# 3x3 convolution of two bottleneck layers: last row tile by F(2,3), three of six row combinations with four products per two columns, differences on GpSimd, statistics on ScalarE

## The chip, the cores and the metric

The kernel runs on one core of a Trainium2 chip. The metric is the time of one execution on the device in microseconds, the median of several runs; lower is better. Everything is float32. TensorE (PE) does the matrix products, VectorE (DVE) element work between tiles, ScalarE (ACT) function evaluations and copies, GpSimd (POOL) slow element work, and SyncE (SP) issues transfers.

## The reference

Two residual bottleneck layers in a row, on an input of 64 images, 1024 channels, 14 x 14 pixels:

```
for layer in range(2):
    h = relu(bn(conv1x1(x, w1) + b1))        # 1024 -> 256 channels
    h = relu(bn(conv3x3(h, w2, pad=1) + b2)) # 256 -> 256
    h = bn(conv1x1(h, w3) + b3)              # 256 -> 1024
    x = relu(x + softplus(residual_scale) * h)
```

`bn` takes mean and variance of each channel over all 64 x 14 x 14 pixels of the batch. So no value of a layer's next step can be made before all images of the step ahead are done and their statistics are known.

## The kernel before

The stages follow each other: conv1 of layer 0 (to about 310 us), the 3x3 convolution of layer 0 (to 655), a Gram stage that derives the statistics of conv3 from a matrix of inner products (to 773), conv3 of layer 0 fused with conv1 of layer 1 (to about 1380), the 3x3 convolution of layer 1 (to about 1730), its Gram stage, and conv3 with the residual to the end. Within a stage each engine works through its own list in a fixed order that a scheduler sets when the program is built; engines wait for each other by semaphores. The results of conv1 and conv2 stay in SBUF as one tensor `y`, 128 partitions x 2 halves of the channels.

The change lies in the 3x3 convolution, `conv2`, and in `filters`, which prepares its weights. `conv2` computes in place over `y`, in NG = 8 groups of GI = 8 images. It is a Winograd scheme in both directions:

- Rows: the 14 output rows are cut into RT = 4 tiles of four rows, the last with two that count. F(4,3) makes four output rows from NF = 6 *combinations* i of input rows. `combine` builds them on VectorE (tiles `r`), the fourth tile's row with help from ScalarE (`last`, L420). They are handled in pairs: (1,2), then (3,4), then (0,5). A combination has 4 x 8 = 32 lines of 14 columns, combination 5 only 24.
- Columns: F(2,3) with five products per two output columns. Even and odd columns are kept as two halves of a line. `sums` (L437) holds the two halves added. In `products`, L494 multiplies `sums` with the shared weight D1D2 into one PSUM bank, and L513 multiplies the halves with D1, D3, D2 and D0 into two more. Each of these exists for two halves of the input channels and two of the output channels: 20 products to a combination. One float32 product is two rows in the trace.
- `finish`: ScalarE copies the shared bank to `ms` (L535, or L531 with the bias for combination 1). VectorE adds it to the two other banks (`column`, L541), giving `f`, then builds output rows from the six `f` by the inverse row transform (L563 to L583), writes them over `y`, and takes batch statistics of each row tile (`bn_stats`, L555). `summarize` and `aggregate` join the statistics of all groups.

The loop over pairs issues the row combinations of the next pair ahead of the products of this one:

```
now, ahead = ahead, combine(*pairs[k + 1]) if k + 1 < len(pairs) else None
acc = finish(g, pair, products(now, k == 0), acc)
```

PSUM has eight banks and all serve this stage in turn, three to a combination, so a bank is taken again after eight takings, when its last reader is done. The transformed weights `u` of a combination come from DRAM for every group by SyncE's queue, three buffers deep. `norm` (L401) applies conv1's normalization and relu to the next group on ScalarE.

`filters(b, s, o, spare)` transforms one quarter of the 3x3 weights of layer b and writes the six sets to DRAM by GpSimd's queue. Layer 0's four quarters are done beside conv1 of layer 0, layer 1's beside the Gram stage of layer 0.

Of the kernel before, what the change touches and what calls it, by code (L numbers as in the profile page):

```python
# [34 lines left out]
P = 128  # L36
# [21 lines left out]
RT, NF, NK = 4, 6, 5  # L58
LINE = GI * W
BUFS = dict(u=3, t=3, r=4, sums=4, ms=3, f=2)  # L60
D0, D1D2, D3, D1, D2 = range(NK)
# [11 lines left out]
def bottlenecks(ctx: ExitStack, tc: tile.TileContext, x, w1s, w2s, w3s, pars, out):  # L73
# [10 lines left out]
        [dram.tile([P, MS, MS, NK, P], FP, tag=f"u{b}_{i}", name=f"u{b}_{i}") for i in range(NF)] for b in range(2)  # L84
# [61 lines left out]
    def filters(b, s, o, spare):  # L146
# [13 lines left out]
        n = NK * P  # L160
        for i in range(NF):

            u = second[:, (i - 1) * n : i * n] if 0 < i < NF - 1 else first[:, 3 * w :][:, (2 * w if i == 0 else 0) :]
            u = u[:, :n].rearrange("p (k m) -> p k m", k=NK)
            r = u[:, 0:3, :].rearrange("p k m -> p (k m)")
            if i in (0, NF - 1):
                nc.scalar.activation(r, g[:, 0 if i == 0 else 2], AF.Copy, scale=0.25 if i == 0 else 1.0)
            else:
                base, by = ((even, -1.0 / 6), (even, 1.0 / 6), (quad, 1.0 / 12), (quad, -1.0 / 12))[i - 1]
                nc.vector.scalar_tensor_tensor(r, g[:, 1], by, base, ALU.mult, ALU.add)  # L170
            nc.vector.tensor_sub(
                u[:, D1 : D2 + 1], u[:, D0 : D3 + 1 : D3 - D0], u[:, D1D2 : D1D2 + 1].to_broadcast([P, 2, P])
            )
            nc.gpsimd.dma_start(out=us[b][i][:, s, o], in_=u)
# [233 lines left out]
    def conv2(psum, pool, b, par, aff, stats):  # L408
        pairs = [(g, p) for g in range(NG) for p in ((1, 2), (3, 4), (0, NF - 1))]
# [15 lines left out]
        def combine(g, pair, between=None):  # L425


            full = RT - 1
# [3 lines left out]
            def ready(r):  # L432
                i = pair[len(made)]
                lines = (full if i == NF - 1 else RT) * GI
                r = r.rearrange("p s r (i w) -> p s (r i) w", i=GI)[:, :, :lines]
                sums = pool.tile([P, MS, RT * GI, WH], FP, tag="sums", name="sums", bufs=BUFS["sums"])[:, :, :lines]
                nc.vector.tensor_add(sums, r[:, :, :, WH:], r[:, :, :, :WH])  # L437
                u = pool.tile([P, MS, MS, NK, P], FP, tag="u", name="u", bufs=BUFS["u"])
                nc.sync.dma_start(out=u, in_=us[b][i])
                made.append((i, lines, r, sums, u))  # L440

            both = slice(0, MS)
            if pair[0] == 1:
                t1, t2 = new("t"), new("t")
                slots = [both] if between is None else [slice(s, s + 1) for s in range(MS)]
                for part in slots:
                    if part.start:
                        between()
                    last(t1, g, 2, -4.0, part)
                    last(t2, g, 1, -4.0, part)  # L450
# [4 lines left out]
                ready(ra)  # L455
                nc.vector.tensor_sub(rb, t1, t2)
                ready(rb)
            elif pair[0] == 3:
                t3, t4 = new("t"), new("t")
                last(t3, g, 2, -1.0)  # L460
                last(t4, g, 1, -1.0)
                for t, k in ((t3, 4), (t4, 3)):
                    ins = nc.vector.tensor_sub(
                        t[:, :, :full], rows(g, both, k, 0, full), rows(g, both, k - 2, 0, full)
                    )
                    if g == 0:
                        tc.keep_in_program_order(ins)
                stt(ra, t4, 2.0, t3)
                ready(ra)
                stt(rb, t4, -2.0, t3)  # L470
                ready(rb)
            else:
                last(ra, g, 2, -5.0)
                for s in range(MS):
                    stt(ra[:, s, :full], rows(g, s, 2, 0, full), -5.0, rows(g, s, 4, 0, full))
                    stt(rb[:, s, :full], rows(g, s, 3, 0, full), -5.0, rows(g, s, 5, 0, full))
                for s in range(MS):
                    stt(ra[:, s, 1:], rows(g, s, 0, 1, RT), 4.0, ra[:, s, 1:])
                    stt(rb[:, s, :full], rows(g, s, 1, 0, full), 4.0, rb[:, s, :full])
                ready(ra)  # L480
                ready(rb)
            return made

        def products(made, first):
# [3 lines left out]
            for i, lines, r, sums, u in made:  # L488
                n = lines * WH
                m = psum.tile(2 * RT * GI * WH).rearrange("p (o n) -> p o n", o=MS)  # L490
                eos = [psum.tile(2 * RT * GI * WH).rearrange("p (q n) -> p q n", q=2) for o in range(MS)]

                def shared(o, s):
                    nc.tensor.matmul(  # L494
                        m[:, o, :n], u[:, s, o, D1D2], sums[:, s].rearrange("p l c -> p (l c)"),
# [3 lines left out]
                def columns(o, s, part):  # L499

                    odd, even = (eos[o][:, q, :n].rearrange("p (l c) -> p l c", c=WH) for q in range(2))
                    to, k, v = (
# [13 lines left out]
                if by_slot:  # L516
                    order = [(s, o, part) for s in range(MS) for o in range(MS) for part in range(4)]
                    order += [(s, o, None) for o in range(MS) for s in range(MS)]
                else:
                    order = [  # L520
                        (s, o, part) for o in range(MS) for part in (None, 0, 1, 2, 3) for s in range(MS)
                    ]
                for s, o, part in order:
                    if part is None:
                        shared(o, s)
                    else:
                        columns(o, s, part)
# [6 lines left out]
                else:  # L534
                    nc.scalar.activation(ms[:, :, :n], m[:, :, :n], AF.Copy)  # L535
# [421 lines left out]
```

## Time and profile before

| | |
|---|---|
| median of 3 runs | 2176.95 us (2176.35 to 2179.06) |
| profiled execution, its own time | 2176.9 us |
| its span | 2175.1 us |
| 3x3 convolution of layer 0, about | 310 to 655 us |
| Gram stage of layer 0, about | 655 to 773 us |
| 3x3 convolution of layer 1, about | 1380 to 1730 us |

A profile row names the source line, the engine, the operation, the written and read tiles, and the shapes. Busy times of engines overlap, so they don't add up to the span. What a change in a stage is worth is read from which engine has no gaps there.

### The profile page before, as it was taken

Reading aid. Unit: us, or ns where it says so; the run is one execution under the profiler, and the core shown is the slowest. Engines: PE = TensorE matmul, PEld = TensorE weight load, DVE = VectorE, ACT = ScalarE, POOL = GpSimd, SP = SyncE. Lnnn points to the kernel's source line nnn. Section 1 sums busy time; section 2 is a strip of 40 time slices with the busy share of each in tenths; the row PEclk is TensorE's granted clock in tenths of the full one; section 3 lists DMA queues with packets and bytes.
Section 4 is the critical chain, followed back from the end, with each engine's and each line's share of the span. In section 5 each row is a group of like instructions: output and inputs, shape, how many; then the busy total and the mean of one; then the engine's idle time right before and its main releaser. Section 6 shows DMA issues by size and latency. Waiting matters only on the chain.

```text
span 2175.1 us, 27250 instructions
## 1 busy us (share of the span) xinstructions
PE 2123.2 (98%) x10624; PEld 1802.2 (83%) x10624; DVE 1432.1 (66%) x2648; ACT 720.8 (33%) x1387; POOL 243.6 (11%) x342
## 2 busy tenths in 40 slices
PE   8999989999998999999999999899999899999999
PEld 4555559999997879999999999899999897555555
DVE  5666567788775667667667666778878634444444
ACT  1111124111105045555555555611111221444444
POOL 0000000000001123333333333000000000000000
PEclk9999999999999999999999999999999999999999
DMA  7655524555544434444444443355555411777885
GB/s 285 252 203 208 177 102 173 190 194 194 192 147 164 156 119 167 164 174 171 160 174 178 178 171 126 151 194 194 188 181 194 185 47 53 303 296 292 299 300 233
DMA packets 45010, 409.45 MB, mean 188 GB/s; under 512 B 5584, under 2 KB 5840, under 8 KB 12240
## 3 DMA queue, kind: packets, MB, share of 16 engines
q1 hardware_dynamic: 30528, 288.67, 36.8%
q0 software_dynamic: 8448, 67.11, 7.5%
q10 hardware_dynamic: 5904, 51.91, 5.8%
q8 instruction: 84, 1.38, 0.3%
q14 instruction: 46, 0.38, 0.1%
HBM read 289.18 MB, written 118.49 MB: 187 GB/s over the span
## 4 chain that ended last, share of the span: by engine, by line
PE 93%; DVE 3%; DMA 1%; ACT 1%; issue 0%; POOL 0%; SPq 0%; DVEq 0%; ACTq 0%
PE ps L513 23%; PE ps L144 17%; PE ay L144 15%; PE cy L144 8%; PE ap L144 8%; PE ps L494 6%; PE ax L144 4%; PE cp L144 4%; PE cp L622 4%; PE cx L144 2%; PE ap L623 2%; PE ps L640 1%; DMA y<-in_w 1%; DVE spare L170 0%; ACT y L401 0%
## 5 line engine op out<-in xcount | busy, mean ns | idle before, releaser
L513 PE MATMUL ps<-r,u 128*128 128x224 f32 (+3 forms) x3072 | 561.3, 334 | 14.1 <-DVE r L454 14.1
L513 PEld LDWEIGHTS ps<-r,u 128*128 128x128 f32 x3072 | 535.1, 189 | 19.8 <-DVE r L454 7.9
L144 PE MATMUL ps<-y,w 128*128 128x392 f32 x1024 | 339.5, 494 | 0.0
L144 PEld LDWEIGHTS ps<-y,w 128*128 128x128 f32 x1024 | 195.4, 191 | 143.0 <-issue 1.9
L704 DVE SCALAR_TENSOR_TENSOR x<-ps,scale,x 128x392 f32<-128x392 f32 x256 | 160.1, 626 | 174.4 <-PE ps L144 174.4
L239 ACT ACTIVATE cu<-cy,scale 128x196 f32<-128x196 f32 x372 | 154.0, 423 | 221.2 <-PE cy L144 221.2
L705 ACT ACTIVATE x<-x,shift 128x392 f32<-128x392 f32 x264 | 163.7, 622 | 182.8 <-DVE x L704 182.8
L144 PE MATMUL ay<-at,w1s 128*128 128x196 f32 (+1 forms) x752 | 209.7, 382 | 1.2 <-ACT au L239 1.0
L541 DVE TENSOR_TENSOR f<-ps,ms 128x448 f32<-128x448 f32 x192 | 111.2, 598 | 128.4 <-PE ps L513 73.7
L494 PE MATMUL ps<-sums,u 128*128 128x224 f32 (+1 forms) x768 | 169.7, 344 | 0.0
L535 ACT ACTIVATE ms<-ps 128x448 f32<-128x448 f32 (+1 forms) x80 | 42.0, 525 | 382.6 <-PE ps L494 382.6
L144 PEld LDWEIGHTS ay<-at,w1s 128*128 128x128 f32 x752 | 136.0, 190 | 36.6 <-ACT au L239 4.6
L239 ACT ACTIVATE x<-x,shift 128x392 f32<-128x392 f32 x248 | 140.9, 614 | 27.9 <-POOL x L373 27.9
L373 POOL TENSOR_TENSOR x<-x,cu 128x392 f32<-128x392 f32 x124 | 125.9, 1015 | 187.6 <-DVE x L347 187.6
L347 DVE SCALAR_TENSOR_TENSOR x<-cp,scale,x 128x196 f32<-128x196 f32 x248 | 103.5, 417 | 63.7 <-PE cp L144 63.7
L494 PEld LDWEIGHTS ps<-sums,u 128*128 128x128 f32 x768 | 136.5, 189 | 0.1
L622 PE MATMUL cp<-zt 128*128 128x257 f32 x392 | 119.9, 387 | 6.5 <-DVE zt L642 6.2
L144 PE MATMUL cy<-ct,w3s 128*128 128x196 f32 x496 | 123.0, 330 | 1.4 <-ACT cu L239 1.4
L239 ACT ACTIVATE au<-ay 128x196 f32<-128x196 f32 (+1 forms) x141 | 53.8, 381 | 178.4 <-PE ay L144 175.8
L144 PE MATMUL ap<-x,w1s 128*128 128x196 f32 (+1 forms) x376 | 107.7, 390 | 4.9 <-DVE y L285 4.9
L401 ACT ACTIVATE y<-y,shift,scale 128x1568 f32<-128x1568 f32 (+2 forms) x68 | 103.1, 1585 | 5.6 <-DVE shift L801 5.6
L144 PE MATMUL ay<-x,w 128*128 128x196 f32 (+1 forms) x376 | 104.8, 381 | 0.0
(188 smaller groups left out, 3056.5 us busy)
## 6 DMA issues: line engine op xcount, KB each, us to landing
u<-u SPq DMA_DIRECT2D x96, 1280.0 KB, 5.5
x<-in_x SPq DMA_DIRECT2D x62, 1568.0 KB, 6.7
x<-mid SPq DMA_DIRECT2D x32, 1568.0 KB, 8.6
mid<-x ACTq DMA_DIRECT2D x31, 1568.0 KB, 5.1
out<-x POOLq DMA_DIRECT2D x31, 1568.0 KB, 7.7
u<-y POOLq DMA_DIRECT2D x24, 320.0 KB, 6.6
u<-spare POOLq DMA_DIRECT2D x24, 320.0 KB, 3.1
y<-in_w SPq DMA_DIRECT2D x4, 576.0 KB, 8.7
```

Of the source, the lines that this page charges most:

```text
L144: tc.keep_in_program_order(nc.tensor.matmul(*args, **kw))
L239: tc.keep_in_program_order(nc.scalar.activation(*args, **kw))
L347: nc.vector.scalar_tensor_tensor(v, bank, self.scale[:, o : o + 1], v, ALU.mult, ALU.add)
L373: nc.gpsimd.tensor_add(v, v, self.u12)
L401: nc.scalar.activation(y, y, AF.Relu, bias=shift[:, s : s + 1], scale=scale[:, s : s + 1])
L494: nc.tensor.matmul(m[:, o, :n], u[:, s, o, D1D2], sums[:, s].rearrange("p l c -> p (l c)"), start=(s == 0), stop=(s == MS - 1),)
L513: nc.tensor.matmul(to, u[:, s, o, k], v, start=start, stop=stop, skip_group_check=by_slot)
L541: nc.vector.tensor_tensor(f[:, o].rearrange("p r (i q c) -> p q (r i) c", i=GI, q=2)[:, :, :lines], eos[o][:, :, :n].rearrange("p q (l c) ...
L622: nc.tensor.matmul(g0, zt[:, c, 0:P], zt[:, c, :], start=first, stop=last)
L623: nc.tensor.matmul(g1, zt[:, c, P:M], zt[:, c, P:], start=first, stop=last)
L704: nc.vector.scalar_tensor_tensor(v, ps, scale[:, o : o + 1], v, ALU.mult, ALU.add)
L705: nc.scalar.activation(v, v, AF.Relu, bias=shift[:, o : o + 1])
```

## The change

1. The last row tile, of which two rows count, is made by F(2,3) instead of F(4,3). It needs combinations 0, 1, 2 and 5 only, so combinations 3 and 4 have 24 lines now, and combination 5 has 32. The factors of `last` change, and the fourteenth output row is written apart (L671).
2. Combinations 3, 4 and 5 (`FOUR`) use a column scheme with four products per two columns: weights D0M2, SUM, DIFF and D3M1. `sums` goes with SUM, a new operand `diffs` with DIFF, and a new operand `v` with the other two, always over all seven columns of a half. That is 16 products (32 rows) instead of 20 (40 rows), and four PSUM banks instead of three (`less` beside `m` and the two of `eos`). `diffs` is made by GpSimd (L478); `v` by two operations of VectorE (L482) and two of ScalarE for the end columns (L486, L487). In `finish`, `shared_part` (L619) writes `m - ms` and `m + ms` to `f` by two operations of VectorE before the columns (L627) are added.
3. Statistics: groups 0 and 7 keep `bn_stats`. For groups 1 to 6, ScalarE reads the finished group twice per channel half with an accumulated output (`moment`, L700: Identity and Square around a center that group 0 gives), after the pairs (1,2) and (3,4) of the next group. `merge` and `begin` bring the three parts into six entries.
4. The last pair is handled as (5, 0).
5. `filters` makes the four weights of `FOUR` combinations by more and smaller operations, and these sets have 1024 KB instead of 1280.

```
-        pairs = [(g, p) for g in range(NG) for p in ((1, 2), (3, 4), (0, NF - 1))]
+        pairs = [(g, p) for g in range(NG) for p in ((1, 2), (3, 4), (NF - 1, 0))]
...
-                lines = (full if i == NF - 1 else RT) * GI
+                lines = (full if i in (3, 4) else RT) * GI
...
                 nc.vector.tensor_add(sums, r[:, :, :, WH:], r[:, :, :, :WH])
+                if i in FOUR:
+                    diffs = half("diffs")
+                    nc.gpsimd.tensor_sub(diffs, r[:, :, :, :WH], r[:, :, :, WH:])
+                    v = pool.tile([P, MS, RT * GI, W], FP, tag="v", name="v", bufs=BUFS["v"])[:, :, :lines]
+                    for s in range(MS):
+                        q = r[:, s].rearrange("p l (q c) -> p l q c", q=2)
+                        nc.vector.tensor_sub(
+                            v[:, s, :, 1 : W - 1].rearrange("p l (q c) -> p l q c", q=2),
+                            q[:, :, :, 1:], q[:, :, :, : WH - 1],
+                        )
+                    nc.scalar.activation(v[:, :, :, 0], r[:, :, :, 0], AF.Copy)
+                    nc.scalar.activation(v[:, :, :, W - 1], r[:, :, :, W - 1], AF.Copy, scale=-1.0)
+                    r = v
...
+                if four:
+                    for to, k, v in ((less, DIFF, diffs), (m, SUM, sums)):
+                        for o, s in each:
+                            shared(to, k, v, o, s)
+                    for o in range(MS):
+                        for part in range(2):
+                            for s in range(MS):
+                                columns(o, s, part)
...
+        def shared_part(item, f):
+            four, lines, m, ms, eos = item
+            if four:
+                a, l = (v[:, :, : lines * WH].rearrange("p o (l c) -> p o l c", c=WH) for v in (m, ms))
+                for q, op in enumerate((ALU.subtract, ALU.add)):
+                    nc.vector.tensor_tensor(halves(f, lines)[:, :, q], a, l, op)
...
+        def moment(g, o, k):
+            nc.scalar.activation(
+                idle, y_all[:, o, g * GPX : (g + 1) * GPX], (AF.Identity, AF.Square)[k], bias=center[:, o : o + 1],
+                accum_out=moments[:, o, k, g - 1 : g],
+            )
...
+            if g > 1 and pair[0] in (1, 3):
+                for i in range(2):
+                    moment(g - 1, (1, 3).index(pair[0]), i)
...
+            if i in FOUR:
+                r0, r1, r2 = (row[:, k * P : (k + 1) * P] for k in range(3))
+                ends = rest[:, w : w + P]
+                nc.vector.tensor_add(ends, r0, r2)
+                nc.vector.tensor_add(u[:, SUM], ends, r1)
+                nc.vector.tensor_sub(u[:, DIFF], ends, r1)
+                nc.scalar.activation(u[:, SUM : DIFF + 1], u[:, SUM : DIFF + 1], AF.Copy, scale=0.5 * by)
+                nc.scalar.activation(u[:, D0M2], r0, AF.Copy, scale=-by)
+                nc.scalar.activation(u[:, D3M1], r2, AF.Copy, scale=by)
```

What follows is the order of instructions on an engine at three places, without times. First TensorE: one output half of combination 3 or 4 before.

```order
L494 MATMUL ps<-sums,u 128x224 x2
L513 MATMUL ps<-r,u 128x224 x2
L513 MATMUL ps<-r,u 128x32x6 x2
L513 MATMUL ps<-r,u 128x224 x2
L513 MATMUL ps<-r,u 128x32x6 x2
```

And after, for the whole combinations 3, 4 and 5 in turn:

```order
L550 MATMUL ps<-diffs,u 128x168 x4
L550 MATMUL ps<-sums,u 128x168 x4
L560 MATMUL ps<-v,u 128x168 x8
L550 MATMUL ps<-diffs,u 128x168 x4
L550 MATMUL ps<-sums,u 128x168 x4
L560 MATMUL ps<-v,u 128x168 x8
L550 MATMUL ps<-diffs,u 128x224 x4
L550 MATMUL ps<-sums,u 128x224 x4
L560 MATMUL ps<-v,u 128x224 x8
```

The shared products, of `diffs` and of `sums`, now stand ahead of all column products of a combination instead of ahead of each output half's.

Second VectorE, in the finish of the pair (3, 4) of an early group. Before (L541 is `column`, L456 the combination 4 of the next group, L423 the two-operand form `stt`):

```order
L541 TENSOR_TENSOR f<-ps,ms 128x2x32x7 x2
L456 TENSOR_TENSOR r<-t 128x896
L568 TENSOR_TENSOR fc<-f 128x896
L569 TENSOR_TENSOR fd<-f 128x896
L423 SCALAR_TENSOR_TENSOR y<-fc,fa 128x3x112
L423 SCALAR_TENSOR_TENSOR y<-fd,fb 128x4x112 x2
L423 SCALAR_TENSOR_TENSOR y<-fc,fa 128x3x112
L423 SCALAR_TENSOR_TENSOR fb<-fd,fb 128x2x336
L573 TENSOR_TENSOR fa<-fa,fc 128x896
L555 BN_STATS stats_0_1195<-y 128x6 x4
```

After (L619 is the shared part, L482 `v` of combination 5, L627 `column`):

```order
L475 TENSOR_TENSOR sums<-r 128x448
L619 TENSOR_TENSOR f<-ps,ms 128x2x24x7 x2
L482 TENSOR_TENSOR v<-r 128x32x12 x2
L627 TENSOR_TENSOR f<-ps,f 128x2x24x7 x2
L513 TENSOR_TENSOR t<-y 128x2x336
L619 TENSOR_TENSOR f<-ps,ms 128x2x24x7 x2
L475 TENSOR_TENSOR sums<-r 128x448
L627 TENSOR_TENSOR f<-ps,f 128x2x24x7 x2
L457 SCALAR_TENSOR_TENSOR r<-t 128x2x336
L652 TENSOR_TENSOR fc<-f 128x2x336
L653 TENSOR_TENSOR fd<-f 128x2x336
```

The statistics are gone from this place, and shared parts and `v` stand ahead of the columns.

Third ScalarE, between two groups. Before (L420 are last rows of `t` and `r`, L535 and L531 the copies to `ms`):

```order
L420 ACTIVATE t<-y 128x2x112 x2
L535 ACTIVATE ms<-ps 128x448
L535 ACTIVATE ms<-ps 128x2x168
L531 ACTIVATE ms<-ps,par_134 128x224 x2
L420 ACTIVATE t<-y 128x2x112 x2
L420 ACTIVATE r<-y 128x2x112
```

After (L454 are the last rows, L486 and L487 end columns of `v`, L700 the moments, L605 and L601 the copies):

```order
L605 ACTIVATE ms<-ps 128x448
L486 ACTIVATE v<-r 128x2x24
L487 ACTIVATE v<-r 128x2x24
L454 ACTIVATE t<-y 128x2x112
L700 ACTIVATE idle,moments<-y,center 128x1568
L454 ACTIVATE r<-y 128x2x112
L700 ACTIVATE idle,moments<-y,center 128x1568
L454 ACTIVATE r<-y 128x2x112
L700 ACTIVATE idle,moments<-y,center 128x1568
L601 ACTIVATE ms<-ps,par_134 128x224 x2
L700 ACTIVATE idle,moments<-y,center 128x1568
L605 ACTIVATE ms<-ps 128x448
```

Three moments now stand ahead of the copy of combination 1's shared product, with last rows between them.

More of the change, by code (lines that the diff above doesn't have):

```diff
@@ L83, in bottlenecks @@
     us = [
[L84 removed]
+        [dram.tile([P, MS, MS, NKS[i], P], FP, tag=f"u{b}_{i}", name=f"u{b}_{i}") for i in range(NF)]
+        for b in range(2)
     ]
@@ L160, in filters @@
         n = NK * P
+        rest = first[:, 5 * w + n :]
+        bases = {1: (even, -1.0 / 6), 2: (even, 1.0 / 6), 3: (quad, 1.0 / 12), 4: (quad, -1.0 / 12)}
         for i in range(NF):
[L163 to L167, printed above, removed]
-            else:
-                base, by = ((even, -1.0 / 6), (even, 1.0 / 6), (quad, 1.0 / 12), (quad, -1.0 / 12))[i - 1]
-                nc.vector.scalar_tensor_tensor(r, g[:, 1], by, base, ALU.mult, ALU.add)
```

218 lines of the change are left out of this document (142 added, 76 removed).

## The prediction

> **What bounds the kernel now.** I read the page's totals and its chain first, then one steady group of eight images by stretches of time, then that group's products and vector work one by one, last the waits.
>
> ```profile
> PE 2123.2 (98%) x10624; PEld 1802.2 (83%) x10624; DVE 1432.1 (66%) x2648; ACT 720.8 (33%) x1387; POOL 243.6 (11%) x342
> ...
> PE 93%; DVE 3%; DMA 1%; ACT 1%; issue 0%; POOL 0%; SPq 0%; DVEq 0%; ACTq 0%
> PE ps L513 23%; PE ps L144 17%; PE ay L144 15%; PE cy L144 8%; PE ap L144 8%; PE ps L494 6%; PE ax L144 4%; PE cp L144 4%; PE cp L622 4%; PE cx L144 2%; PE ap L623 2%; PE ps L640 1%; DMA y<-in_w 1%; DVE spare L170 0%; ACT y L401 0%
> ```
>
> TensorE holds 93% of the chain, and the products that the change cuts (L494, L513) hold 29% of it.
>
> ```profile
> core 0: us, PE busy (x) PEld busy (x) DVE busy (x) ACT busy (x) POOL busy (x), PEclk, DMA share, GB/s
> 406.56:448.14 41.58, 41.58 (x242) 41.30 (x241) 33.83 (x59) 5.14 (x12) 0.00 (x0) 1.00 0.53 190
> 310.00:655.00 345.00, 337.70 (x1927) 333.87 (x1926) 276.08 (x486) 67.63 (x117) 0.00 (x0) 0.99 0.50 183
> 655.30:773.00 117.70, 104.73 (x657) 92.63 (x658) 65.45 (x137) 34.45 (x36) 13.10 (x28) 0.95 0.41 148
> ```
>
> The first row is one steady group of the 3x3 convolution. It takes 41.58 us and TensorE has no gap in it; VectorE works 33.83 us, ScalarE 5.14, GpSimd not at all. So each microsecond of products saved is a microsecond of the group, until VectorE stands in the way. Its room is 41.58 - 33.83 = 7.75 us now, and the change shrinks that from above.
>
> ```profile
> DVE f L541 <- PE ps L513: 37.6, 24, 1.7
> DVE f L541 <- ACT ms L535: 26.9, 17, 4.3
> PE ps L513 <- DVE r L454: 7.3, 1, 7.3
> ```
>
> In the whole first 3x3 stage the only large wait of TensorE is the one at its start (7.3 us, once); VectorE is the one that waits, for products and for ScalarE's copy of them.
>
> **TensorE: narrower and fewer products.**
>
> ```profile
> 434.55 0.92 PE L494 MATMUL ps<-sums,u 128*128 128x224 f32 x4
> ...
> 438.16 0.92 PE L494 MATMUL ps<-sums,u 128*128 128x224 f32 x4
> ...
> 441.77 0.73 PE L494 MATMUL ps<-sums,u 128*128 128x168 f32 x4
> 442.34 2.32 PE L513 MATMUL ps<-r,u 128*128 128x168 f32 x16
> 444.50 0.73 PE L494 MATMUL ps<-sums,u 128*128 128x168 f32 x4
> ...
> 447.22 0.92 PE L494 MATMUL ps<-sums,u 128*128 128x224 f32 x4
> ```
>
> From one L494 to the next is one output half of a combination: 20 rows in the trace, 4 of L494 and 16 of L513, half of the latter without the last column. With 32 lines that is 12 x 224 + 8 x 192 = 4224 columns in 3.61 us, 0.855 ns a column; with 24 lines 12 x 168 + 8 x 144 = 3168 columns in 2.73 us, 0.862. A group is now 5 x 7.22 + 5.45 = 41.6 us, as the window says.
>
> After, combinations 0, 1 and 2 keep 7.22 us each. Combinations 3 and 4 have 24 lines and 32 full rows: 32 x 168 x 0.862 = 4.63 us each. Combination 5 has 32 lines and 32 rows: 32 x 224 x 0.855 = 6.13. Sum 21.7 + 9.26 + 6.13 = 37.08, so 4.51 us less a group and **72.2 us** less over 16 groups (eight in each layer).
>
> **VectorE: what is swapped.** Time from start to start in the same group:
>
> ```profile
> 412.73 1.14 DVE L541 TENSOR_TENSOR f<-ps,ms 128x448 f32<-128x448 f32 x2
> 413.80 0.91 DVE L423 SCALAR_TENSOR_TENSOR r<-y 128x336 f32<-128x336 f32 x2
> 414.63 0.92 DVE L423 SCALAR_TENSOR_TENSOR r<-y,r 128x336 f32<-128x336 f32 x2
> ...
> 422.25 1.08 DVE L564 TENSOR_TENSOR fb<-f 128x896 f32<-128x896 f32 x1
> 423.26 0.50 DVE L423 SCALAR_TENSOR_TENSOR r<-y 128x336 f32<-128x336 f32 x1
> ...
> 440.20 0.85 DVE L423 SCALAR_TENSOR_TENSOR fb<-fd,fb 128x672 f32<-128x672 f32 x1
> 440.97 1.08 DVE L573 TENSOR_TENSOR fa<-fa,fc 128x896 f32<-128x896 f32 x1
> ```
>
> 448 elements take 1.07 / 2 = 0.535 us, 336 take 0.415, 896 take 1.01, 672 take 0.77. That is 1.04 ns an element and 0.07 us, so 288 would be 0.37, 384 0.47, 224 0.30. Per steady group the change removes eight statistics (4 x 0.535 + 4 x 0.415 = 3.80). It adds the differences `v` (4 x 0.37 + 2 x 0.47 = 2.42), the shared parts of L619 (4 x 0.415 + 2 x 0.535 = 2.73), the fourteenth row apart (0.30), and a wider sum and columns of combination 5 (0.36). Three rows instead of four in combinations 3 and 4 and in what is built from them take off some 2.16. Net -0.15: about 33.7 us of work in a group of 37.08. Nine tenths busy, still not the bound.
>
> Does its order hold up TensorE? In the order of after, VectorE's tightest stretch begins with the second column of combination 2, which can't run before TensorE has ended that combination, 14.46 us into the group. Behind it stand r, fa, fb, sums, combination 3's shared part and combination 5's `v`; by the pitches above these are done at about 19.4 and 20.3. TensorE, with four banks for a combination of four products instead of three, asks for the bank that this shared part frees at 25.25, and for `v` at 26.8. Slack 5.9 us. In group 0 of each layer the statistics stay on VectorE and L619 and `v` come on top, so it needs 39 us and hands group 1 a lateness of 2 to 5 us, less than that slack. I take 1 us for both layers (0 to 6).
>
> **GpSimd: the differences.** Two operands of 336 elements twice and of 448 once per group. The fused stage has the nearest rows:
>
> ```profile
> L373 POOL TENSOR_TENSOR x<-x,cu 128x392 f32<-128x392 f32 x124 | 125.9, 1015 | 187.6 <-DVE x L347 187.6
> L368 POOL TENSOR_TENSOR x<-x,cu x124: 596/600/1117, 786.5 to 1366.2; 128x196 f32<-128x196 f32 x124
> ...
> 786.18 0.96 DVE L312 TENSOR_TENSOR at<-x,at 128x784 f32<-128x784 f32 x1
> ...
> 786.49 1.12 POOL L368 TENSOR_TENSOR x<-x,cu 128x196 f32<-128x196 f32 x1 [2.07 <-ACT cu L239]
> ```
>
> 196 elements take 0.600 us and 392 take 1.015: 2.1 ns an element and 0.19 us, so 2 x 0.90 + 1.13 = 2.93 us a group. The result is wanted a pair of combinations later, so GpSimd's own time is hidden by products. But the last two rows show one add starting inside a VectorE operation with two inputs in SBUF, and taking 1.12 instead of 0.60. The two engines can hold each other up, so VectorE may lose anything from 0 to those 2.93 us; at the worst 33.7 + 2.9 = 36.6, still under 37.08. Nothing in the sum, but no room left: this is the first rival.
> [...]
>
> **ScalarE: the statistics.**
>
> ```profile
> L401 ACT ACTIVATE y<-y,shift,scale 128x1568 f32<-128x1568 f32 x58 | 93.9, 1684 | 2.8 <-DVE shift L801 2.8
> L420 ACT ACTIVATE t<-y 128x224 f32<-128x224 f32 x60 | 20.0, 381 | 64.2 <-DVE r L456 55.6 <-DVE r L423 8.6
> ```
>
> The four moments of a group have the size of L401's row, 93.9 / 58 = 1.62 us each, and the end columns of `v` are small, like L420 (six a group, 0.3 to 0.4). 5.14 + 6.5 + 2 is some 13 to 14 us of 37. What matters is the queue: three moments stand between the last-row copies that VectorE needs and combination 1's `ms`. From the moment U that allows the first, the copy for combination 5 ends at about U + 4.7 and VectorE reaches it at U + 5.7; `ms` comes at U + 6.7, VectorE's column at U + 6.5. Cost 0.2 us of VectorE, none of TensorE.
>
> **Weights and the stages beside.**
>
> ```profile
> u<-u SPq DMA_DIRECT2D x45, 1280.0 KB, 5.5
> ...
> PE cp L622 <- DVE zt L642: 6.2, 5, 1.6
> L171 DVE TENSOR_TENSOR spare<-spare 128x256 f32<-128x256 f32 x24 | 9.0, 417 | 1.4 <-ACT spare L167 1.4
> ...
> 652.97 2.32 PE L513 MATMUL ps<-r,u 128*128 128x168 f32 x16
> 661.33 1.30 PE L640 MATMUL cy<-ident,y 128*128 128x128 f32 x4 [6.05 <-ACT y L401]
> ```
>
> A load of weights lands in 5.5 us, three buffers give it more than 9 us, and those of four products have a fifth less to bring: nothing. The filters are transformed beside other stages, layer 0's four pieces in the first, layer 1's in the Gram stage (655 to 773 us). Each piece gets six more operations of VectorE (three of 128 elements for one of 256, +0.8 us) and eight small copies of ScalarE more (+2.2 us). In the Gram stage TensorE already waits for VectorE five times, 6.2 us in all: +2 us there (0 to 4 x 3.0 = 12, if all were exposed), +0.5 in the first. After the last product TensorE has 6.05 us of nothing while statistics end; the last item is now 448 wide instead of 336, three operations longer by 0.12 each: +0.4 a layer, +0.8.
>
> **Sum.** The profiled execution took 2176.9 us (span 2175.1), the same as the median. 2176.9 - 72.2 + 1 + 2.5 + 0.8 = **2109 us**. By ends: without the added terms 2105, with them all at their upper ends 2124.
>
> **Rivals.**
> 1. *VectorE becomes the bound.* The differences read at a stride, the adds of the fused stage don't. If they take 1.12 / 0.60 = 1.87 times as long and block VectorE throughout, it needs 33.7 + 5.5 = 39.2, which is 2.1 over TensorE. Seven boundaries give 14.8 less 5.9 slack, so about 9 a layer: 2127; with half of the blocking it stays at 2109. For it speaks the 1.12 row; against it that blocking in full needs every difference to lie beside VectorE work of two SBUF inputs.
> 2. *The change loses (the other side).* The same lock, but each difference holds VectorE over 2.6 us: (41.6 - 33.7) / 3 is the point from which a group is longer than now. At 3.0 us a group is 42.7: 2176.9 + 1.1 x 16 + 4 = 2199. Against it: 2.6 us is more than twice the slowest add, 1.12.
> 3. *The narrow products gain less.* If rows of 168 were paced by their weight loads, 32 x 0.188 = 6.02 us instead of 4.63, the saving falls to 1.73 a group, 27.7 in all: 2153. Against it:
>
> ```profile
> L513 PEld LDWEIGHTS ps<-r,u x3072: 187/188/338, 319.6 to 1724.7; 128*128 128x128 f32 x192
> 442.20 2.24 PEld L513 LDWEIGHTS ps<-r,u 128*128 128x128 f32 x16
> ```
>
> One load lasts 188 ns, but sixteen beside rows of 168 and 144 take 2.24 us, 140 ns each: they overlap.
> 4. *The filters are exposed.* Each piece holds up its stage for its whole 3.0 us, in both stages: +24 less the 2.5 taken: up to 2130.
>
> **Chances.** The forecast 0.70, with a range of its own of 2104 to 2116; the first rival 0.18; the filters 0.06; weight loads 0.03; the loss 0.03. All but the last are faster by more than 0.2% (4.4 us, about what a measurement of this kernel can tell from no change); a partial loss that ends within it gets 0.01. 2102 to 2130 holds all but the third and the second rival; its low end lets the narrow rows run at 0.855 ns a column (1.2 us less) and leaves room for the spread of the runs (2176.35 to 2179.06).
>
> **What would show it.** Right: a group period near 37.1 us with TensorE at 97% or more; the L550 and L560 rows of 168 columns at 0.145 us each; differences of 0.9 to 1.15 us; moments at 1.6; the Gram stage within 2 us of 117.7. Wrong: in the 3x3 stages TensorE waits for shared parts or `v`, VectorE busy above 95%, L619 or `v` much over 0.42 us beside GpSimd's work (first rival); narrow rows at 0.188 (third); more than 10 us of waits for `zt` in the Gram stage (fourth).

## The result, and the profile after

The changed kernel takes 2128.55 us (median of four runs, 2126.36 to 2129.66) against 2176.65 before; the ratio is 0.9775 with a 95% interval of 0.9758 to 0.9792. That is 48.1 us less where 68 were forecast. The profiled execution took 2126.36 us, its span 2124.6, which is 50.5 less than the span before.

First the page of after, the lines that answer to those of before, and the new GpSimd group (count, then busy time and mean ns of one, then idle time before it):

```profile
PE 2058.2 (97%) x10240; PEld 1733.5 (82%) x10240; DVE 1466.6 (69%) x2826; ACT 823.3 (39%) x1627; POOL 355.5 (17%) x390
...
PE 92%; DVE 5%; ACT 2%; issue 1%; DMA 1%; POOL 0%; DVEq 0%; POOLq 0%; ACTq 0%; SPq 0%
...
L478 POOL TENSOR_TENSOR diffs<-r 128x336 f32<-128x336 f32 (+1 forms) x48 | 112.1, 2337 | 622.4 <-DVE r L457 394.0
```

TensorE is busy 65.0 us less (2123.2 to 2058.2), and VectorE and ScalarE together have gained three points of the chain. The differences take 2.34 us each on the average, more than twice the 0.98 that was forecast.

Next, where the time went. These are the starts of the stages in the timeline of after, then of before; L863 and L730 are the same line, the first VectorE work for conv3:

```profile
344.78 8.44 PE L573 MATMUL ps<-r,u 128*128 128x224 f32 x32 [7.30 <-DVE r L506]
649.25 1.40 PE L773 MATMUL cy<-ident,y 128*128 128x128 f32 x4 [6.12 <-ACT y L427]
L863 DVE TENSOR_TENSOR ct<-ct,y x31: 356/410/412, 758.2 to 1330.8; 128x196 f32<-128x196 f32 x31
1376.86 7.82 PE L573 MATMUL ps<-r,u 128*128 128x224 f32 x32 [6.80 <-DVE r L506]
1679.36 1.39 PE L773 MATMUL ps<-ident,y 128*128 128x128 f32 x4 [4.77 <-ACT y L427]
```

```profile
319.62 8.74 PE L513 MATMUL ps<-r,u 128*128 128x224 f32 x32 [7.30 <-DVE r L454]
L730 DVE TENSOR_TENSOR ct<-ct,y x31: 354/410/413, 773.1 to 1344.8; 128x196 f32<-128x196 f32 x31
1390.81 7.36 PE L513 MATMUL ps<-r,u 128*128 128x224 f32 x32 [6.81 <-DVE r L454]
1729.89 1.39 PE L640 MATMUL ps<-ident,y 128*128 128x128 f32 x4 [4.79 <-ACT y L401]
```

Subtracting neighbours (the Gram stage of layer 0 began at 661.33 before) gives this table, in us:

| stage | before | after | difference |
|---|---|---|---|
| conv1 of layer 0, to the first product of the 3x3 | 319.6 | 344.8 | +25.2 |
| 3x3 of layer 0, with its tail | 341.7 | 304.5 | -37.2 |
| Gram stage of layer 0 | 111.8 | 109.0 | -2.8 |
| fused conv3 and conv1 | 617.7 | 618.7 | +1.0 |
| 3x3 of layer 1, with its tail | 339.1 | 302.5 | -36.6 |
| the rest | 445.2 | 445.2 | 0.0 |

So the 3x3 stages gave 73.8 us, and conv1 of layer 0, which the change touches only through the filter pieces beside it, took 25 of them back.

One steady group of after, on TensorE (start, duration, then the instruction and how many in a row):

```profile
435.70 1.30 PE L550 MATMUL ps<-diffs,u 128*128 128x168 f32 x8
436.84 1.30 PE L550 MATMUL ps<-sums,u 128*128 128x168 f32 x8
437.98 2.48 PE L560 MATMUL ps<-v,u 128*128 128x168 f32 x16
440.30 1.30 PE L550 MATMUL ps<-diffs,u 128*128 128x168 f32 x8
...
444.89 1.67 PE L550 MATMUL ps<-diffs,u 128*128 128x224 f32 x8
...
450.98 0.92 PE L550 MATMUL ps<-sums,u 128*128 128x224 f32 x4
```

A combination of 24 lines takes 440.30 - 435.70 = 4.60 us (forecast 4.63) and combination 5 takes 450.98 - 444.89 = 6.09 (6.13). The windows over four groups of after and five of before, in the columns of the prediction's window, say how full the engines are:

```profile
444.89:592.70 147.81, 147.81 (x866) 146.91 (x865) 138.76 (x255) 48.14 (x99) 33.63 (x12) 1.00 0.54 193
```

```profile
406.56:614.46 207.90, 207.90 (x1202) 206.51 (x1201) 170.12 (x293) 25.44 (x59) 0.00 (x0) 1.00 0.52 190
```

147.81 / 4 = 36.95 us a group against 41.58, with TensorE still without a gap. VectorE works 34.7 us of that (34.0 of 41.58 before), ScalarE 12.0.

Now the stage that became longer. TensorE, with what it waited for, then its waits in the first 330 us:

```profile
47.60 2.80 PE L155 MATMUL ay<-at,w 128*128 128x392 f32 x8
55.13 5.17 PE L155 MATMUL ay<-at,w1s 128*128 128x392 f32 x8 [4.74 <-ACT au L265]
60.14 2.80 PE L155 MATMUL ax<-x,w 128*128 128x392 f32 x8
```

```profile
PE ay L155 <- ACT au L265: 19.5, 5, 4.7
```

`au` (L265) is ScalarE's copy of a bank that TensorE is to go on using. It comes 4.74 us late once for each of the four filter pieces. ScalarE's own list at that place shows why, and then VectorE's:

```profile
50.77 0.29 ACT L193 ACTIVATE y<-y 128x128 f32<-128x128 f32 x1
53.33 0.42 ACT L191 ACTIVATE y<-y 128x256 f32<-128x256 f32 x1 [2.27 <-DVE y L190]
53.99 0.31 ACT L192 ACTIVATE y<-y 128x128 f32<-128x128 f32 x1 [0.25 <-DVE y L183]
54.21 0.49 ACT L193 ACTIVATE y<-y 128x128 f32<-128x128 f32 x2
54.61 0.47 ACT L265 ACTIVATE au<-ay 128x392 f32<-128x392 f32 x1
```

```profile
51.11 1.78 DVE L338 TENSOR_TENSOR at<-x,at 128x1568 f32<-128x1568 f32 x1
52.81 0.28 DVE L189 TENSOR_TENSOR y<-y 128x128 f32<-128x128 f32 x1
53.01 0.28 DVE L190 TENSOR_TENSOR y<-y 128x128 f32<-128x128 f32 x1
53.40 0.56 DVE L183 SCALAR_TENSOR_TENSOR y<-y 128x384 f32<-128x384 f32 x1
```

TensorE had filled the bank at about 50.4. But ahead of `au` in ScalarE's list stood L191, a small copy of a filter, which waited 2.27 us for VectorE's L190, and that stood behind a sum `at` of 1.78 us. Then came L192 and two L193, of which the first two needed L183. L183 writes the scratch that both combinations use, so it stands behind L190, the last of VectorE's sums that read it for the combination ahead. `au` itself waited for nothing by 54.61; it was only behind.

The stall cost more than its length: the eight products after it took 5.17 us instead of the 2.80 of the next eight. The windows over the stall and over these products have the reason, in the third number from the end, the granted clock:

```profile
50.30:55.10 4.80, 0.10 (x1) 0.00 (x0) 4.59 (x11) 2.03 (x8) 1.32 (x3) 0.77 0.95 345
55.10:60.50 5.40, 5.37 (x10) 2.90 (x11) 1.10 (x4) 1.07 (x3) 1.08 (x2) 0.57 0.77 242
```

Over the stretch behind the stall the granted clock was 0.57, and 0.50 in its first 2.9 us. So a piece cost about 4.7 us of waiting and 2.4 us of slow products.

### The profile page after: what moved, and what is told of

It is laid out like the page before. It is cut to its first block, busy times and chain, and to the rows that moved or that the text cites. A ratio compares the mean times of both kernels' runs of the same rounds, so it can differ in the third digit from the quotient of the medians.

```text
span 2124.6 us, 27204 instructions
## 1 busy us (share of the span) xinstructions
PE 2058.2 (97%) x10240; PEld 1733.5 (82%) x10240; DVE 1466.6 (69%) x2826; ACT 823.3 (39%) x1627; POOL 355.5 (17%) x390
## 4 chain that ended last, share of the span: by engine, by line
PE 92%; DVE 5%; ACT 2%; issue 1%; DMA 1%; POOL 0%; DVEq 0%; POOLq 0%; ACTq 0%; SPq 0%
PE ps L155 17%; PE ay L155 15%; PE ps L573 13%; PE ps L550 9%; PE cy L155 8%; PE ap L155 7%; PE ps L560 6%; PE ax L155 4%; PE cp L155 4%; PE cp L755 3%; PE cx L155 2%; PE ap L756 2%; ACT y L427 1%; PE ps L773 1%; DVE at L319 0%
## 5 line engine op out<-in xcount | busy, mean ns | idle before, releaser
L573 PE MATMUL ps<-r,u 128*128 128x224 f32 (+1 forms) x1536 | 294.0, 343 | 14.1 <-DVE r L506 14.1
L573 PEld LDWEIGHTS ps<-r,u 128*128 128x128 f32 x1536 | 279.6, 191 | 18.1 <-DVE r L506 7.9
L265 ACT ACTIVATE cu<-cy,scale 128x196 f32<-128x196 f32 x372 | 153.7, 422 | 221.7 <-PE cy L155 221.7
L155 PE MATMUL ay<-at,w1s 128*128 128x196 f32 (+1 forms) x752 | 219.1, 396 | 20.0 <-ACT au L265 20.0
L478 POOL TENSOR_TENSOR diffs<-r 128x336 f32<-128x336 f32 (+1 forms) x48 | 112.1, 2337 | 622.4 <-DVE r L457 394.0
L155 PEld LDWEIGHTS ay<-at,w1s 128*128 128x128 f32 x752 | 140.3, 196 | 59.7 <-ACT au L265 23.4
L550 PE MATMUL ps<-sums,u 128*128 128x224 f32 (+1 forms) x768 | 156.0, 337 | 0.0
L265 ACT ACTIVATE x<-x,shift 128x392 f32<-128x392 f32 x248 | 140.8, 614 | 27.9 <-POOL x L399 27.9
L605 ACT ACTIVATE ms<-ps 128x448 f32<-128x448 f32 (+1 forms) x80 | 40.4, 505 | 265.5 <-PE ps L550 256.4
L560 PE MATMUL ps<-v,u 128*128 128x168 f32 (+1 forms) x768 | 130.9, 322 | 0.0
L265 ACT ACTIVATE au<-ay 128x196 f32<-128x196 f32 (+1 forms) x141 | 53.6, 380 | 184.5 <-PE ay L155 184.1
L560 PEld LDWEIGHTS ps<-v,u 128*128 128x128 f32 x768 | 123.5, 188 | 0.8
```

The costliest lines, as they stand in the source:

```text
L155: tc.keep_in_program_order(nc.tensor.matmul(*args, **kw))
L265: tc.keep_in_program_order(nc.scalar.activation(*args, **kw))
L478: nc.gpsimd.tensor_sub(diffs, r[:, :, :, :WH], r[:, :, :, WH:])
L550: nc.tensor.matmul(to[:, o, :n], u[:, s, o, k], v[:, s].rearrange("p l c -> p (l c)"), start=(s == 0), stop=(s == MS - 1),)
L560: nc.tensor.matmul(to, u[:, s, o, k], v, start=(s == 0), stop=(s == MS - 1))
L573: nc.tensor.matmul(to, u[:, s, o, k], v, start=start, stop=stop, skip_group_check=by_slot)
```

## The experiments

**The filters of the kernel before.** This asks whether the 25 us are the filters at all.

```
-            if i in FOUR:
-                r0, r1, r2 = ...
-                ... (six operations)
+            nc.vector.tensor_sub(u[:, D1 : D2 + 1], u[:, D0 : D3 + 1 : D3 - D0], ...)   # for every i
+            u = u[:, : NKS[i]]
```

> The filter transform of the kernel before, for all six combinations and both layers; of the five planes that it makes for combinations 3, 4 and 5 only the first four are stored, so the weights of these three are not those of the four products and the output isn't the convolution. Everything else as after. Theory (ScalarE's queue in the first stage: the copies L191 to L193 stand ahead of `au`, which TensorE waits for): the first product of the 3x3 stage of layer 0 comes at about 319 us instead of 344.8, and the time falls by 25 us to about 2102. Rival (the first stage is longer for another reason than the filters, such as the clock or the loads): it stays at 2125 to 2130. In the Gram stage the pieces are the old ones too: if the new ones gave its gain of 2.8 us, it goes back to 112 us from first transpose to fused stage, and the time is 2105.

2104.72 us, ratio 0.9665 (0.965 to 0.9679). The weights that it stores for combinations 3, 4 and 5 aren't those of the four products, so only its times are of use. The first product of the 3x3 stage:

```profile
320.56 8.52 PE L564 MATMUL ps<-r,u 128*128 128x224 f32 x32 [7.30 <-DVE r L497]
```

It is 24.2 us earlier than in after, so the first shift comes from the filter pieces. The Gram stage is back at 736.6 - 625.2 = 111.4 us, and the time fits the 2105 of the second half of the expectation. But the cause of that second shift isn't shown: the row change alone, further below, has the old filter transform too, and its Gram stage takes 114.4 us.

**A scratch of their own.** Is it the shared scratch, or any copy ahead of `au`?

```
-        rest = first[:, 5 * w + n :]
+        rests = {3: first[:, 5 * w + n :], 4: second[:, 4 * n :], 5: second[:, 2 * n + 4 * P : 3 * n]}
```

> Combinations 3, 4 and 5 get a scratch of their own in the filter transform, so VectorE doesn't wait for ScalarE's copies of the combination ahead; the copies stay on ScalarE. Theory (any of these copies ahead of `au` costs, since each waits for VectorE): part of the delay stays, each of the four waits for `au` falls from 4.7 to 1 to 4 us, time 2105 to 2122. Rival (the exchange of VectorE and ScalarE over one shared scratch is the whole cause): the waits vanish, time about 2102.

2113.2 us, ratio 0.9707 (0.9693 to 0.9722), 15 us better than after and inside the first range of the expectation. Its 3x3 stage begins at 326.49, 18.3 us earlier than in after; its Gram stage takes 114.3 us, 5.3 more. Its waits in the first 320 us, the products behind one of them, and the window there:

```profile
PE ay L155 <- ACT au L265: 7.7, 5, 1.8
...
53.70 2.90 PE L155 MATMUL ay<-at,w1s 128*128 128x392 f32 x8 [1.77 <-ACT au L265]
...
52.10:57.00 4.90, 3.30 (x10) 2.01 (x11) 4.69 (x12) 3.33 (x11) 2.13 (x4) 1.00 0.98 355
```

Each wait falls from 4.74 to about 1.8 us, not to nothing. With a scratch of its own the second L183 follows the first at once, and no L191 stands ahead of `au` any more: the shared scratch, with the order that it forced on both lists, was some 3 us of the wait, the copies that still stand ahead of `au` the rest. With 1.77 us of idle time the clock stays at 1.00 and eight products take 2.90 us. The shorter stall pays twice.

**The copies on VectorE, and on GpSimd.** Same operations, other queues (L191 to L193).

```
-                nc.scalar.activation(u[:, SUM : DIFF + 1], u[:, SUM : DIFF + 1], AF.Copy, scale=0.5 * by)
+                nc.vector.tensor_scalar(u[:, SUM : DIFF + 1], u[:, SUM : DIFF + 1], 0.5 * by, None, ALU.mult)
                 ... (L192 and L193 alike; nc.gpsimd in the second)
```

> The three copies with a factor (L191 to L193) are made by VectorE instead of ScalarE, nine more small operations of VectorE for a piece, some 2 us; scratch shared as after. Theory (ScalarE's queue): no wait for `au` of more than 1 us, first stage at 319 to 322 us, time 2101 to 2105. Rival (the amount of added work holds up the stage, whoever does it): VectorE's own sums `at` come later by those 2 us and more, TensorE waits for them instead, 4 x 2 to 4 x 5 us stay: 2110 to 2125.

> The same three copies on GpSimd, which is idle in the first stage but for issuing the stores of the weights; scratch shared as after, so VectorE waits for GpSimd between combinations. Theory (ScalarE's queue): no wait for `au`, but VectorE's queue may now hold a filter operation that waits for GpSimd ahead of an `at` or a `y`: 2101 to 2108. Rival (the exchange over one scratch is the cause, whichever engine makes the copies): GpSimd is slower than ScalarE, VectorE waits longer, and TensorE waits for `at` or `y`: 2120 to 2140.

On VectorE 2108.63 us, ratio 0.9685 (0.9671 to 0.97); on GpSimd 2099.28 us, ratio **0.964** (0.9624 to 0.9656), the fastest kernel of this study, 29 us ahead of after. All waits of TensorE for `au` in the GpSimd version, over the whole span, and the start of its 3x3 stage:

```profile
PE ay L155 <- ACT au L265: 1.0, 2, 0.6
```

```profile
318.23 8.82 PE L573 MATMUL ps<-r,u 128*128 128x224 f32 x32 [7.30 <-DVE r L506]
```

That is 26.5 us earlier than after. That it is 1.4 earlier than before too says little: the six kernels here that have these copies on GpSimd begin the stage between 317.69 and 320.70. On VectorE it began at 320.50, within that spread, so the amount of added work isn't what held it up. VectorE's version missed its upper expectation by 3.6 us in the Gram stage, which grew to 739.7 - 624.4 = 115.3 us, against 109.0 with GpSimd: TensorE waited 7.5 us for `zt` there, 2.8 with GpSimd. GpSimd is slower than ScalarE, as its rival had it: an add of 392 elements took 1.02 us in the fused stage before, ScalarE's copy of 392 above 0.47. But the long waits of TensorE for `y` did not come: 5.8 us in four waits, 3.9 in three in after.

The next kernels start from the GpSimd version, so that the first stage doesn't blur them; in the one without four products these copies don't occur.

**The differences on VectorE.** This tests the first rival of the prediction.

```
-                    nc.gpsimd.tensor_sub(diffs, r[:, :, :, :WH], r[:, :, :, WH:])
+                    nc.vector.tensor_sub(diffs, r[:, :, :, :WH], r[:, :, :, WH:])
```

> As e4_copies_on_gpsimd (2099.3 us), but the three differences of a group (L478) are made by VectorE: 2 x 0.415 + 0.535 = 1.37 us more in its list, GpSimd has none. Theory (where the two engines meet, GpSimd is the one that is held up, and VectorE loses nothing): VectorE goes from 34.1 to 35.5 us of a group of 36.95, TensorE still sets the pace, the groups stay at 36.95 and the time within 3 us of 2099. Rival (GpSimd's differences also cost VectorE time, the first rival of the prediction, so that taking them away frees it): VectorE's busy time doesn't rise by 1.37 but stays or falls, and waits of TensorE, if any, go; time the same or up to 3 us less. The busy time of VectorE in a steady group tells these apart, not the total.

2101.23 us, ratio 0.9652 (0.9637 to 0.9666): no difference from 2099.28 that the intervals tell. VectorE over four groups of this kernel (the row of after above, 138.76 us, is also that of the kernel with the differences on GpSimd); then the operation `fa` (L646) over four groups of after, and of this kernel:

```profile
419.85:567.67 147.82, 147.82 (x867) 146.92 (x866) 141.14 (x268) 48.54 (x100) 0.00 (x0) 1.00 0.55 193
```

```profile
L646 DVE TENSOR_TENSOR fa<-f 128x896 f32<-128x896 f32 x4 | 8.2, 2058 | 0.0
```

```profile
L646 DVE TENSOR_TENSOR fa<-f 128x896 f32<-128x896 f32 x4 | 4.3, 1085 | 0.0
```

Neither theory holds alone. VectorE rises by 0.60 us a group, not 1.37: the differences on GpSimd had cost it 0.8 us net, and the one `fa` that took 2.06 instead of 1.09 is enough to account for that. The timeline of after shows both directions of this, GpSimd first, then VectorE:

```profile
421.83 0.92 POOL L478 TENSOR_TENSOR diffs<-r 128x336 f32<-128x336 f32 x1 [19.75 <-DVE r L457]
...
474.10 1.41 POOL L478 TENSOR_TENSOR diffs<-r 128x448 f32<-128x448 f32 x1 [13.31 <-PE ps L550]
484.46 5.40 POOL L478 TENSOR_TENSOR diffs<-r 128x336 f32<-128x336 f32 x1 [8.95 <-DVE r L457]
```

```profile
421.61 0.61 DVE L627 TENSOR_TENSOR f<-ps,ms 128x448 f32<-128x448 f32 x1
422.14 0.97 DVE L475 TENSOR_TENSOR sums<-r 128x336 f32<-128x336 f32 x1
...
473.40 1.08 DVE L508 TENSOR_TENSOR r<-t 128x896 f32<-128x896 f32 x1
474.39 2.06 DVE L646 TENSOR_TENSOR fa<-f 128x896 f32<-128x896 f32 x1
...
488.22 0.84 DVE L657 TENSOR_TENSOR fa<-fa,fc 128x672 f32<-128x672 f32 x1
488.99 1.14 DVE L619 TENSOR_TENSOR f<-ps,ms 128x448 f32<-128x448 f32 x2
490.06 0.49 DVE L475 TENSOR_TENSOR sums<-r 128x336 f32<-128x336 f32 x1
```

At 421.83 a difference of 336 elements takes 0.92 us. It starts beside L627, which has an operand in PSUM; L475 behind that, with both inputs in SBUF, takes 0.97 us where it takes 0.49 at 490.06. The difference that starts at 484.46, inside a run of VectorE operations with both inputs in SBUF, ends at 489.86, 0.87 us after VectorE has reached L619, which has an operand in PSUM. At 474.10 the difference started inside L508, which has both inputs in SBUF too, came ahead of `fa`, and `fa` waited for it: it ended at 476.45, 0.94 us after the difference, and took 2.06 us for 1.09. So in each of these places one of the two engines waited. But at 484.46 the wait went on past the end of the operation that was running (L652, to 485.1): GpSimd got no turn for 4.5 us between eight operations that follow each other without a gap, while between L508 and `fa`, which follow each other just so, it got one. What decides this the runs don't show.

**The statistics back on VectorE.**

```
-            to = {0: first_stats, NG - 1: stats[:, :, 1:]}.get(g)
+            to = stats[:, :, PARTS * g : PARTS * (g + 1)]        # all groups
-            if g > 1 and pair[0] in (1, 3):  ... moment(...)
```

> As e4_copies_on_gpsimd, but the statistics of all groups are taken by VectorE with bn_stats (6 x 0.415 + 2 x 0.30 + 2 x 0.535 = 4.16 us a group), no moments on ScalarE; 40 entries are joined at the end, about 1 us more there. Theory (VectorE has 2.8 us of room in a group and 5.9 of slack in a layer): 38.3 us of work in a group of 36.95, lateness grows by 1.3 a group, 7 x 1.3 - 5.9 = 3 us a layer, and the time is 2105 to 2112. Rival (VectorE doesn't bind, since TensorE takes its operands long before): 2098 to 2102.

2116.95 us, ratio 0.9725 (0.9709 to 0.9741): 17.7 us slower than with ScalarE's moments, more than the 6 to 13 expected. The window over four groups (the third busy time is VectorE's), a wait late in the layer, and the start of the Gram stage:

```profile
417.71:568.02 150.31, 148.56 (x867) 146.72 (x865) 150.31 (x288) 23.60 (x68) 21.79 (x12) 1.00 0.54 189
```

```profile
558.73 1.41 PE L550 MATMUL ps<-diffs,u 128*128 128x168 f32 x8 [0.52 <-POOL diffs L478]
...
630.59 1.39 PE L766 MATMUL cy<-ident,y 128*128 128x128 f32 x4 [11.13 <-ACT y L427]
```

VectorE is busy all the time. The first groups still come at 36.95 us, and 568.02 - 529.57 = 38.45 us later in the layer. Most of the price is at the end: VectorE reaches the last rows late, and the wait before the Gram stage is 11.1 us instead of 6.2, and 10.8 instead of 4.8 in layer 1. The expectation had left this tail out.

**The row change without four products.**

```
-FOUR = 3, 4, 5
+FOUR = ()
```

> Of the change only the last row tile by F(2,3), the order (5, 0) and the statistics on ScalarE: no combination uses four products, so there is no diffs, no v, no shared part, and the filters are made as before. Theory (the time of the 3x3 stage is that of its products): a group is 4 x 7.22 + 2 x 5.45 = 39.8 us instead of 36.95, the time 2176.9 - 1.8 x 16 = 2148 less about 2 for what the stages beside gave. Rival (part of the gain comes from VectorE's lighter list, statistics gone to ScalarE): lower than 2140.

2151.46 us, ratio 0.9878 (0.9864 to 0.9893). Combination 3 in two neighbouring groups:

```profile
415.97 0.73 PE L550 MATMUL ps<-sums,u 128*128 128x168 f32 x4
...
455.77 0.73 PE L550 MATMUL ps<-sums,u 128*128 128x168 f32 x4
```

39.80 us a group, as forecast. The two 3x3 stages lose 14.5 and 14.1 us, so the row change, with the order (5, 0) and the statistics on ScalarE, is worth 28.6 us, and four products instead of five the other 45.2 of the 73.8. The total is 5 us above the 2146 of the expectation: 2.6 are the Gram stage (114.4 us), the remainder small shifts in other stages.

**Four products for combination 0 too.**

```
-FOUR = 3, 4, 5
+FOUR = 0, 3, 4, 5
+                shared_part(done[1], fb)      # ahead of the columns of combination 0
```

> As e4_copies_on_gpsimd, with combination 0 of four products too: its products fall from 7.22 to 6.13 us, VectorE gets two shared parts and two v more (2 x 0.535 + 2 x 0.47 = 2.0 us). Theory (VectorE has 2.8 us of room): 36.1 us of VectorE in 35.86 of products, VectorE becomes the bound in the long run, but within a layer the slack of 5.9 us covers 7 x 0.25; time 2099.3 - 1.09 x 16 + 0 to 5 = 2082 to 2087. Rival (VectorE's order holds up TensorE when it is full, as every wait for a shared part or v then reaches TensorE): groups of 37 us and more, 2095 to 2110.

2121.63 us, ratio 0.9745 (0.9731 to 0.976): 22 us slower than without it, though its products are some 17 us shorter. The rival had the direction, and a price that was still too low. Window over four groups, and the wait before the Gram stage:

```profile
424.37:571.65 147.28, 144.36 (x834) 142.03 (x833) 144.15 (x261) 49.84 (x108) 29.32 (x16) 1.00 0.52 186
```

```profile
635.08 1.39 PE L774 MATMUL cy<-ident,y 128*128 128x128 f32 x4 [13.04 <-ACT y L427]
```

36.82 us a group, of which VectorE works 36.0 and TensorE 36.1: neither has room, and the layers end with 13.0 and 12.3 us of waiting instead of 6.2 and 4.8. Within a layer TensorE waits little for shared parts (1.7 us in all), which the rival had named. Its longest waits, 10.9 us in seven, stand ahead of products of combination 1. The profile names no releaser for them, but the times do; here is one of them with VectorE's row:

```profile
510.11 0.99 PE L550 MATMUL ps<-sums,u 128*128 128x224 f32 x4 [1.08 <-issue]
509.40 0.61 DVE L475 TENSOR_TENSOR sums<-r 128x448 f32<-128x448 f32 x1
```

All seven products start 0.71 or 0.72 us after VectorE has started the `sums` that they read, which its full list has made late.

**Part of `v` on GpSimd.** The same kernel, relieved of two and of four operations.

```
-                        nc.vector.tensor_sub(v[:, s, :, 1 : W - 1]...
+                        (nc.gpsimd if i in (0,) else nc.vector).tensor_sub(...    # then i in (0, 5)
```

> As e8_five_of_six (2121.6 us; VectorE the bound, e4_copies_on_gpsimd 2099.3), but the two operations for the middle of `v` of combination 0 (L482) go to GpSimd. Theory (both engines exclude each other wherever VectorE has two SBUF operands, and VectorE has such work nearly all the time): GpSimd's two operations are blocked behind runs of VectorE like the differences (2 to 5 us each), VectorE loses some 0.5 us of the 0.94 that it is relieved of, groups stay near 36.8 and the time is 2112 to 2122, still slower than e4. Rival (0.94 us less brings VectorE under the 35.86 us of the products): 2083 to 2095.

> As e9, with the middle of `v` of combination 5 on GpSimd too, 1.88 us of VectorE's list moved in all. Theory (exclusion): GpSimd now has seven blocked operations a group, and TensorE waits for `v` or for differences directly: 2105 to 2125. Rival (VectorE alone is the bound, and what is taken from it counts in full): VectorE at some 35 us, 2082 to 2090, the fastest of all.

2110.83 us, ratio 0.9693 (0.9676 to 0.971), and 2108.12 us, ratio 0.9678 (0.9661 to 0.9695). Both are better than 2121.63 and neither reaches the 2099.28 of three combinations. In the second, late groups come at 608.28 - 572.47 = 35.81 us, the pace of the products, but on the way TensorE waited for the operations of shared parts (9.9 us in 6 waits), and the layers end with 8.4 and 7.6 us of waiting. The expectation for e9 was a little too high. Its theory, that the two engines exclude each other wherever VectorE has two operands in SBUF, gave each operation of `v` on GpSimd 2 to 5 us; from 420 to 570 us they took 1.20 us on the average in the first kernel and 1.43 in the second, so blocking of that length was not shown for them. For e10 the expectation held in its time but not in its reason, since in the main it wasn't `v` or differences that TensorE waited for.

## Why the prediction was right, and which step of it failed

The direction and the range held (2102 to 2130), but 2109 was 19.6 us too low. The profiled execution lies 17.4 above it, and one term makes more than all of that: the first stage took 25.2 us more where 0.5 was forecast. The 3x3 stages gave 3.4 us more than forecast (73.8 for 72.2 - 1 - 0.8), the Gram stage took 4.8 less (-2.8 for +2), and the fused stage cost 1.0. So the range held by luck in part: with the error of the first stage alone the time would have been about 2134.

*The products* (-72.2 forecast): 4.63 us a group measured for 4.51, 74.1 over 16 groups. The narrow products run no slower for their weight loads (32 rows of 168 columns in 4.60 us, 0.144 each), so the third rival falls. The two terms for lateness of group 1 (+1) and for the longer tail (+0.8) did not come: in the 3x3 stages of after TensorE waited for no shared part and no `v`, and the wait behind the last product is 6.12 us for 6.05 in layer 0 and 4.77 for 4.79 in layer 1.

*VectorE* (33.7 us a group forecast): 34.7, of which 0.97 is the `fa` held up by GpSimd. The bookkeeping of operations was right, and so was the remark that VectorE might lose up to 2.9 us. That the two engines hold each other up, the mechanism of the first rival, is there, but at 0.8 us a group net; the larger part fell on GpSimd (8.4 us a group for 2.93), which had time. What remained of VectorE's room, 2.3 us, is real: 4.16 us more for statistics or 2.0 for a fourth combination of this form made the kernel slower.

*GpSimd* (2.93 us a group): a difference of 336 elements took 0.92 us where VectorE didn't hold it up, near the 0.90 forecast, so the stride that the first rival feared cost nothing. But it was 33.63 / 4 = 8.4 us a group as it ran, and the mean of 2.34 us lies far outside the 0.9 to 1.15 that was to show the prediction right. It was hidden, as forecast.

*ScalarE* (13 to 14 us a group): 12.0. The three moments ahead of combination 1's `ms` showed no wait of TensorE.

*The filters* are the step that failed. The prediction said "Each piece gets six more operations of VectorE [...] and eight small copies of ScalarE more (+2.2 us)" and took +0.5 us for the first stage and +2 for the Gram stage. Measured: +25.2 in the first, all of which goes when the copies leave ScalarE (26.5 us on GpSimd), and -2.8 in the Gram stage. The copies were priced by duration, where their place in ScalarE's list was what mattered: each waits for VectorE, and `au`, for which TensorE waits, stood behind them. The prediction walked ScalarE's queue through the 3x3 stage for just this effect and did not walk it in the first stage. The fourth rival named the right cause, but at 3.0 us a piece, where a piece cost 25.2 / 4 = 6.3; its 2130 came near only because it counted eight pieces, and the four in the Gram stage cost nothing. It left out that the wait is longer than the work, and that after 4.74 us of idle time TensorE ran at a granted clock of 0.50 for 2.9 us. Why the Gram stage became shorter stays open: TensorE's waits for `zt` fell from 6.2 to 3.0 us and lie between 2.6 and 7.5 over these kernels, but the two kernels above with the old filter transform have 5.8 us of them each, and Gram stages of 111.4 and 114.4.

## What to carry to other kernels

Price an added operation of an in-order engine by what stands behind it in that engine's list and by what it waits for, in every stage where it is issued, and not only in the stage that the change is about. Small copies that nobody is waiting for belong on an engine that, in that stage, issues nothing that TensorE waits for: here the move of three lines from ScalarE to GpSimd was worth 29 us, more than half of the change's own gain. When one engine sets the pace and another is at 94%, expect little more: here the next saving on the first was paid back with interest by the second, much of it at the end of the stage.

## What the runs showed of the hardware that was not expected

- A stall of TensorE of 4.74 us was followed by 2.4 us of loss at a granted clock of 0.57, one of 1.77 us by 0.1 us at a clock of 1.00. How long a stall must be for such a loss, these two don't show.
- GpSimd's operation of 0.92 us lasted 5.40 us beside a run of VectorE operations with both inputs in SBUF that follow each other without a gap. The other way VectorE's `fa` was held in each of four groups (2.06 us for 1.09). In both places GpSimd had started inside the VectorE operation ahead, so the order of the starts alone doesn't tell which of the two waits.
